# A transformer layer on one core: the queries of groups 2 to 6 in one two-level seven-product unit

## The chip, the core and the metric

The kernel runs on one core of a Trainium2 chip. The core has TensorE (PE in the profile; its weight loads are PEld), VectorE (DVE), ScalarE (ACT), GpSimd (POOL) and SyncE (SP), which issues nearly all DMAs here. The metric is device time in microseconds (us) of one execution; less is better.

## What is computed

One decoder layer on 1024 tokens of 512 features, all in fp32: attention with 32 query heads in 8 groups that share keys and values, rotary embedding, a causal softmax, an output projection, a layer norm; then a gated feed-forward part (1792 inner features) and a second layer norm.

```python
q = (x @ wq).reshape(B, T, H, HD).transpose(0, 2, 1, 3)      # T 1024, H 32, HD 128
k = (x @ wk).reshape(B, T, KV, HD).transpose(0, 2, 1, 3)     # KV 8
v = (x @ wv).reshape(B, T, KV, HD).transpose(0, 2, 1, 3)
q = q * cos + _rotate_half(q) * sin
k = k * cos + _rotate_half(k) * sin
scores = jnp.einsum('bhtd,bhsd->bhts', q, k) * (1.0 / np.sqrt(HD))
scores = jnp.where(mask, scores, -jnp.inf)                   # causal
att = jax.nn.softmax(scores, axis=-1)
out = jnp.einsum('bhts,bhsd->bhtd', att, v)
x = _layernorm(x + out.transpose(0, 2, 1, 3).reshape(B, T, H * HD) @ wo)
nx = x * rsqrt(mean(square(x)) + eps) * ln_w
x = _layernorm(x + (silu(nx @ gate_w.T) * (nx @ up_w.T)) @ down_w.T)
```

## The kernel before, in words

**Groups and tiles.** Attention runs group by group (`g`, 0 to 7). A group has four heads and 32 score steps: eight blocks of 128 tokens in the order `ORDER` = 7, 1, 5, 3, 4, 2, 6, 0 (the place in it is `p`), four steps of 32 tokens each (`b`). A step `t` holds 32 tokens of four heads on 128 partitions. `scores` (L590 to L618) multiplies the queries with the keys on PE into one of two PSUM pairs (`pair`, tag `ps_s`, 2 buffers); DVE adds the mask and takes the extreme (L590); ACT takes the exponential into a piece `p` of a pool of ten (L610), after which the pair is free; DVE inverts the sum (L614), ACT scales (L615), DVE transposes blocks of 32 by 32 into the buffer `xs` (L618, `turned` in the profile). After a tile's fourth step, `gather` issues 16 DMAs on SP (L668), which move that tile from `xs` to `ys` (`moved`). Tiles with even `p` use `xs` from its start, those with odd `p` its end. Then `Late` multiplies with the values (o), and for each pair of tiles `project_pair` multiplies with wo in a seven-product form (y), whose sums DVE adds into the result (L773).

**Filling.** All matmuls run in the order written (`keep_in_program_order`). Between two score steps, `run` places other work on PE by a planner's clock `now`, whose unit is a matmul of 512 columns: o and y of earlier tiles (`late`, available from a time `at` that counts the gather's issue and landing), and `early`, the projections of the next group, spread over all 32 steps. The other engines' order comes from a scheduler, unless an instruction is pinned.

**Projections.** `project_two` computes two heads of queries, or two groups' keys or values, for all 1024 tokens: x (features by tokens) is cut in two by features and by tokens, and so are the weights, and seven products of halves, each two matmuls of 512 columns, take the place of eight. Sums of the weights are made on POOL (`weigh`, L281 to L283), sums of x once at the start (s1 to s4). DVE adds the products from PSUM. A group's four query heads are two such steps, 28 matmuls of 512 columns. The rotary embedding follows as `chores` (`rotate_later`): two DVE steps with sin (L412), one with cos and a POOL sum (L417, L418); one chore is run at each score step. Queries lie in three rooms that turn (`held_q`), so that a group's second room can be filled while the first is read.

**The form at two levels in the FFN.** Gate and up projections already use, for units of four feature blocks, the seven-product form inside each of the seven products (`stages`, with `inner_sums` on DVE and `inner` on POOL): 49 matmuls of 256 columns, with copies of partial products from PSUM by ACT (L1440, L1441, L1445, L1448) and adds by DVE (L1458). Three products are interleaved.

**Loads.** `load(s)` brings the weights of step `s` two steps ahead into four buffers (`two_rows`), which the two halves of wo (`load_wo`) share; `weigh_wo` makes their sums on POOL (L315 to L318).

Of the kernel before, what the change touches and what calls it, by code (L numbers as in the profile page):

```python
# [28 lines left out]
F32 = mybir.dt.float32  # L29
BF16 = mybir.dt.bfloat16  # L30
AF = mybir.ActivationFunctionType
ALU = mybir.AluOpType
# [3 lines left out]
P = 128  # L36
# [4 lines left out]
KV = 8  # L41
HD = 128
REP = HEADS // KV
INNER = 1792
NT = T // P
NC = HID // P
NI = INNER // P
W = 512
Q = 32
B = P // Q  # L50
# [42 lines left out]
LEAST = 2  # L93


@with_exitstack
def kernel(
    ctx: ExitStack,
# [30 lines left out]

    cp = pool("cp", 10)  # L130

    ps_s = pool("ps_s", 2, space=PSUM)
    ps_m = pool("ps_m", 4, space=PSUM)

# [52 lines left out]
    with ExitStack() as att:  # L187
# [31 lines left out]
        held_q = qp.tile([P, 3, T // 2 // Q, REP, Q], F32, tag="q", name="queries")  # L219

        wvs, wks, wqs, wos, sums_of = {}, {}, {}, {}, {}
        of_kind = {"q": (wq, wqs), "k": (wk, wks), "v": (wv, wvs)}

        def load_weights(kind, which, parts=1):

            src, of = of_kind[kind]
            n = len(which)
            if kind == "k" and which == [1, 2]:

                t = held_q[:, 2].rearrange("p n h q -> p (n h q)")[:, :T]  # L230
            else:
                t = (rows if n == 1 else two_rows)(f"w{kind}{which[0]}")
            if kind == "k" and which == [KV - 1]:
                t = two_rows("wk_last")[:, :W]
            t = t.rearrange("p (c f) -> p c f", c=NC)
            size = n * HD // parts
            for k in range(parts):
                f0 = which[0] * HD + k * size
                nc.sync.dma_start(
                    t[:, :, k * size : (k + 1) * size],  # L240
                    src[:, f0 : f0 + size].rearrange("(c p) f -> p c f", p=P),
                )
                yield
            if kind == "k":


                with tc.issue_after(added.ins) if which == [1, 2] else ExitStack():
                    nc.gpsimd.tensor_scalar(t, t, -scale, 1.0, ALU.mult, ALU.mult)
            for k, w in enumerate(which):
                of[w] = t[:, :, k * HD : (k + 1) * HD]  # L250
# [18 lines left out]
        def weigh(s):  # L269


            if s >= len(steps):
                return
            kind, *which = steps[s]
            if len(which) < 2 or kind == "q" and which[0] // 2 in PLAIN:
                return
            a, b = (of_kind[kind][1][n] for n in which)
            b11, b21, b12, b22 = a[:, :2], a[:, 2:], b[:, :2], b[:, 2:]
            t = ap.tile([P, 2, NC // 2, HD], F32, tag="uq", name=f"uq{s}")
            u1, u2, u3 = t[:, 0], t[:, 1], b12  # L280
            nc.gpsimd.tensor_tensor(u1, b12, b11, ALU.subtract)  # L281
            nc.gpsimd.tensor_tensor(u2, b22, u1, ALU.subtract)
            nc.gpsimd.tensor_tensor(u3, b22, b12, ALU.subtract)  # L283
            sums_of[s] = b11, b21, b22, u1, u2, u3

        def difference(w):

# [176 lines left out]
        def project_two(s):  # L464


            b11, b21, b22, u1, u2, u3 = sums_of[s]
            u4 = b21
            kind, *which = steps[s]
            u = f"{kind}{which[0]}"  # L470
            v = ap.tile([P, W], F32, tag="v", bufs=1, name=f"sv{u}")

            def out(n, even):

                k = which[n]
                if kind == "q":
                    return queries(k // REP, even)[:, :, k % REP, :]
                if k not in (of := {"k": kTs, "v": vs}[kind]):
                    t = piece(f"{kind}{k}")
                    of[k] = t if kind == "k" else t.rearrange("p (j f) -> p j f", j=NT)  # L480
                t = of[k].rearrange("p (n q) -> p n q", q=P) if kind == "k" else of[k]
                return t[:, 1 - even :: 2, :]

            def done(n, even):

                if kind == "q":
                    rotate_later(out(n, even), even, f"{u}_{n}", even)
                elif kind == "k":
                    rotate_later(out(n, even), even, f"{u}_{n}", 2 * n)

            def put(dst, a, b):
                nc.vector.tensor_tensor(dst, alike(a, dst), b, ALU.add)

            ps = {}
            products = (
                (1, b11, a11), (2, b21, a12), (6, u2, s2), (5, u1, s1), (3, b22, s4),
                (7, u3, s3), (4, u4, a22),
            )
            for k, w, x in products:
                ps[k] = mbank(f"{u}_p{k}")  # L500
                if kind == "v":

                    for j in range(NT // 2):
                        for c in range(NC // 2):
                            matmul(
                                ps[k][:, j * P : (j + 1) * P],
                                lhsT=x[:, c, j * P : (j + 1) * P],
                                rhs=w[:, c],
                                start=c == 0,
                                stop=c == NC // 2 - 1,  # L510
                            )
                        if j == 1:
                            yield 1
                else:
                    for c in range(NC // 2):
                        matmul(
                            ps[k], lhsT=w[:, c], rhs=x[:, c], start=c == 0, stop=c == NC // 2 - 1
                        )
                        if c < NC // 2 - 1:
                            yield 1  # L520
                if k == 1:
                    nc.scalar.copy(v, ps[1])
                elif k == 2:
                    nc.gpsimd.tensor_tensor(u4, b21, u2, ALU.subtract)
                    put(c := out(0, 0), ps[2], alike(v, c))
                    done(0, 0)
                elif k == 6:
                    nc.vector.tensor_tensor(v, ps[6], v, ALU.add)
                elif k == 5:
                    put(c := out(1, 0), ps[5], alike(v, c))  # L530
                elif k == 3:
                    put(c := out(1, 0), ps[3], c)
                    done(1, 0)
                    if s:
                        weigh(s + 1)
                elif k == 7:
                    nc.vector.tensor_tensor(v, ps[7], v, ALU.add)
                    put(c := out(1, 1), ps[5], alike(v, c))
                    done(1, 1)
                else:  # L540
                    put(c := out(0, 1), ps[4], alike(v, c))
                    done(0, 1)
                    if s > 1:
                        load(s + 2)
                yield 1

        def projections(g):
# [6 lines left out]
                pieces += [(NC, project_keys(g, even)) for even in range(2)]  # L554
            for n in (2 * g, 2 * g + 1):
                s += 1
                if n in PLAIN:

                    which = (2, 0), (3, 0), (2, 1)
                    pieces += [(NC, project_queries(g, *which_of)) for which_of in which]  # L560
                else:
                    pieces.append((PAIR * 2, project_two(s)))
# [182 lines left out]
        def project_pair(g, k, oT):  # L745
# [13 lines left out]
            for n, (a, b) in enumerate(products):  # L759
                if n % 2 == 0:  # L760
                    y = mbank(f"y{g}_{k}_{n}").rearrange("p (n f) -> p n f", n=2)
                for h in range(2):
                    matmul(
                        y[:, n % 2, :],
                        lhsT=a[:, h * P : (h + 1) * P],
                        rhs=b[:, h, :],
                        start=h == 0,
                        stop=h == 1,
                    )
                if n % 2 or n == 6:  # L770
                    n0 = n - n % 2
# [10 lines left out]
        class Late:  # L782


            def __init__(self, g, i, y, at, unturned):
# [3 lines left out]
                else:  # L789
                    queue = max(at + TURNED, queue) + ISSUED  # L790
                    self.at = queue + LANDED
                self.g, self.weighed = g, False
                self.place = place(g, ORDER.index(i), i)
                self.left = self.units(g, i)
                self.work = self.pieces(g, i, y, unturned)
# [17 lines left out]
            def pieces(self, g, i, y, unturned):  # L813
# [41 lines left out]
                elif not first and keep:  # L855
                    held.append((PAIR, project_pair(g, k, both[g, k])))
                elif not first:
                    yield from project_pair(g, k, both[g, k])
                    if k == NT // 2 - 1 and g < KV - 2:
                        load_wo(g + 1)  # L860

# [75 lines left out]
        def run(g, until, early, pace, must=0, least=0, limit=None):  # L937
# [22 lines left out]
            while early.done < must:  # L960
                now += early.step()

        sums_of_x = [1, (s3, a11, a21), (s2, s1, a11)]
        for piece_of in (
            project_queries(0, 0, 0),
# [28 lines left out]
        for g in range(KV):  # L994
# [25 lines left out]
            for p, i in enumerate(ORDER):  # L1020
# [6 lines left out]
                    chores[0].append(lambda: nc.vector.tensor_tensor(s4, a12, s2, ALU.subtract))  # L1027
                if g == KV - 1 and p == 1:
                    load_wo(g)
                if g == 0 and 0 < p <= NT // 2:  # L1030
                    with tc.issue_after(cleared.ins):
                        if p == 2:
# [4 lines left out]
                for b in range(B):  # L1037
# [17 lines left out]
                    due += slot * weight[t]  # L1055
                    passed += weight[t]
                    done = p * B + b + 1
                    if g < KV - 2:
                        pace = early.total * min(1, passed / (slots - EARLIER))
                        must = early.total - MOST * max(0, slots - EARLIER - done)  # L1060
                        if g == 0:
# [688 lines left out]
```

## Time and profile before

| | |
|---|---|
| median of 2 runs | 1245.43 us (1245.15 to 1245.72) |
| the profiled execution | 1244.63 us, its span 1242.8 us |
| first scores of groups 1 to 7 | 161.8, 282.0, 403.2, 524.9, 646.1, 767.8, 872.5 us |
| PE busy | 1229.0 us, 99% of the span |
| DVE, ACT, POOL busy | 75%, 42%, 42% of the span |
| granted clock | 0.999 |

Rows of the profile name a line of the kernel, an engine, an operation and its tiles, written as out<-in; "x16" is the number of instructions. An fp32 matmul is two instructions. Line numbers in the groups are those of the kernel before; L137 is the helper through which every matmul goes, so PE's rows are told apart by their tiles: s scores, q_p, k_p and v_p projections, o, y, and in the FFN a, b, ab and c for the units. Matmuls are pipelined: the time of one row is longer than its share of a run of matmuls.

### The profile page before, as it was taken

What the parts mean: (1) busy time and instruction counts of PE and PEld (TensorE: products, weight loads), DVE (VectorE), ACT (ScalarE), POOL (GpSimd) and SP (SyncE); (2) the same over time, 40 slices, a digit from 0 to 9 for tenths busy, and PEclk for the clock granted to TensorE, in tenths of its full rate; (3) what the DMA queues carried; (4) which work ended last, traced back from release to release, by engine and by line L of the source; (5) the groups of instructions that cost most, each with busy time, mean ns of one, the idle gap of its engine ahead of it and who ended that gap; (6) DMA issues with size and microseconds to landing.
All of it is one profiled execution on the core that took longest, in us unless ns stands there. A gap on an engine that the chain in (4) does not pass through costs nothing. (4 is left out here: it accounts for less than half of the span.)

```text
span 1242.8 us, 14956 instructions
## 1 busy us (share of the span) xinstructions
PE 1229.0 (99%) x4336; PEld 770.6 (62%) x4336; DVE 935.2 (75%) x1891; ACT 524.9 (42%) x1075; POOL 516.7 (42%) x749
## 2 busy tenths in 40 slices
PE   9999999999999999999999999999999999999998
PEld 4645576566456755655567556554555758885887
DVE  5876787888788767878787678768766686889755
ACT  0443344444443444344444444544565137673000
POOL 5641334343424233424342424244240667779322
PEclk9999999999999999999999999999999999999999
DMA  8243325433543344434433433443453501140000
GB/s 279 53 117 77 82 63 147 104 83 78 136 106 88 81 130 96 99 80 118 102 94 80 124 92 90 99 126 95 113 117 91 135 18 52 51 136 18 17 18 35
DMA packets 84049, 115.58 MB, mean 93 GB/s; under 512 B 18304, under 2 KB 54912, under 8 KB 83968
## 3 DMA queue, kind: packets, MB, share of 16 engines
q1 hardware_dynamic: 82960, 112.66, 35.5%
q10 hardware_dynamic: 1008, 1.97, 0.4%
q8 instruction: 35, 0.57, 0.2%
q14 instruction: 46, 0.38, 0.1%
HBM read 37.23 MB, written 2.10 MB: 32 GB/s over the span
## 5 line engine op out<-in xcount | busy, mean ns | idle before, releaser
L610 ACT ACTIVATE p<-s,low 128x928 f32<-128x928 f32 (+31 forms) x256 | 179.2, 700 | 374.2 <-DVE low L590 361.9
L618 DVE STREAM_TRANSPOSE turned<-p 128x1024 f32<-128x1024 f32 (+7 forms) x244 | 187.3, 776 | 102.6 <-ACT p L615 68.3
L137 PE MATMUL o<-moved,v 128*128 128x512 f32 x550 | 254.6, 594 | 0.0
L615 ACT ACTIVATE p<-p,share 128x928 f32<-128x928 f32 (+31 forms) x256 | 188.0, 735 | 120.4 <-DVE share L614 120.3
L590 DVE CUSTOM_DVE_ANT_0 s<-s,mask 128x928 f32<-128x928 f32 (+31 forms) x256 | 179.1, 700 | 36.5 <-PE s L137 35.0
L137 PE MATMUL s<-k,queries 128*128 128x512 f32 (+15 forms) x576 | 204.0, 463 | 2.1 <-ACT p L610 2.1
L137 PEld LDWEIGHTS s<-k,queries 128*128 128x128 f32 x576 | 108.4, 190 | 110.5 <-issue 98.1
L137 PEld LDWEIGHTS o<-moved,v 128*128 128x128 f32 x550 | 102.4, 190 | 102.2 <-issue 95.3
L137 PE MATMUL q_p<-blocks,wq 128*128 128x512 f32 x260 | 124.5, 594 | 0.0
L605 POOL MEMSET p<- 128x96 f32 (+2 forms) x192 | 26.9, 151 | 230.4 <-DVE turned L618 209.6
L418 POOL TENSOR_TENSOR queries<-queries,q_b 128x512 f32<-128x512 f32 x52 | 71.5, 1375 | 116.6 <-DVE queries L417 107.7
L137 PE MATMUL y<-wo,oT 128*128 128x256 f32 x428 | 105.0, 382 | 0.7 <-ACT oT L848 0.7
L137 PEld LDWEIGHTS y<-wo,oT 128*128 128x128 f32 x428 | 79.4, 190 | 22.8 <-issue 7.9
L614 DVE RECIPROCAL share<-total 128x1 f32<-128x1 f32 x256 | 40.0, 156 | 61.1 <-ACT p L610 58.9
L412 DVE TENSOR_TENSOR q_b<-queries,sin 64x512 f32<-64x512 f32 x104 | 83.0, 798 | 3.1
L137 PEld LDWEIGHTS q_p<-blocks,wq 128*128 128x128 f32 x260 | 48.4, 190 | 45.9 <-issue 40.0
L137 PE MATMUL s<-kT,queries 128*128 128x512 f32 (+8 forms) x192 | 68.7, 466 | 1.8 <-ACT p L610 1.7
L773 DVE TENSOR_TENSOR sums<-y,sums 128x512 f32<-128x512 f32 x112 | 66.8, 605 | 3.1 <-PE y L137 2.0
L137 PEld LDWEIGHTS s<-kT,queries 128*128 128x128 f32 x192 | 35.7, 190 | 37.6 <-issue 29.2
L137 PE MATMUL y<-u,os 128*128 128x256 f32 x224 | 55.5, 384 | 0.8 <-POOL os L752 0.6
L137 PE MATMUL q_p<-blocks,uq 128*128 128x512 f32 x104 | 49.7, 592 | 0.0
L610 ACT ACTIVATION_READ_ACCUMULATOR p<-s,low 128x1 f32 x256 | 49.4, 193 | 0.0
(350 smaller groups left out, 1986.9 us busy)
## 6 DMA issues: line engine op xcount, KB each, us to landing
moved<-turned SPq DMA_DIRECT2D x112, 128.0 KB, 2.4
moved<-turned SPq DMA_DIRECT2D x128, 112.0 KB, 2.2
moved<-turned SPq DMA_DIRECT2D x112, 96.0 KB, 2.2
moved<-turned SPq DMA_DIRECT2D x112, 80.0 KB, 2.1
wo<-wo SPq DMA_DIRECT2D x16, 512.0 KB, 4.2
moved<-turned SPq DMA_DIRECT2D x128, 64.0 KB, 2.0
wq<-wq SPq DMA_DIRECT2D x14, 512.0 KB, 4.1
moved<-turned SPq DMA_DIRECT2D x128, 48.0 KB, 1.9
```

Source lines behind the costliest of these rows:

```text
L137: tc.keep_in_program_order(nc.tensor.matmul(*args, **kw))
L412: nc.vector.tensor_tensor(alike(b[0], dst)[to], dst[of], alike(sin[:, ts], dst)[of], ALU.mult)
L418: nc.gpsimd.tensor_tensor(dst, dst, alike(b[0], dst), ALU.add)
L590: extreme = nc.vector.tensor_tensor_reduce(out=s[:, :n], in0=s[:, :n], in1=mask[:, T - n :], scale=1.0, scalar=MASKED, op0=ALU.add, op1=AL ...
L605: cleared = nc.gpsimd.memset(p[:, n:full], 0.0)
L610: nc.scalar.activation(p[:, :n], s[:, :n], AF.Exp, bias=low, scale=-1.0, accum_out=total)
L614: nc.vector.reciprocal(share, total)
L615: last_of_all = nc.scalar.activation(p[:, :n], p[:, :n], AF.Copy, scale=share)
L618: nc.vector.transpose(x[:, :, :, b, :].rearrange("p b j q -> p j b q"), p[:, :full].rearrange("p (j b k) -> p j b k", b=B, k=Q),)
L773: pin(nc.vector.tensor_tensor(to, out, to, ALU.add))
```

## The change

Groups 2 to 6 (`UNITS`) no longer have `project_two` steps for their queries. In their place, after the 16th score step of the group before (`done == slots // 2`), `project_unit` computes all four heads in one run of 49 matmuls of 256 columns (seven products at two levels), with at most a few o steps between (`other`). The four inner sums that each of the seven operands of x needs are computed once, in group 0, on POOL (`keep_inner`, 28 sums of 256 columns) and written to DRAM (seven tiles of 128 by 1024). For each unit they are fetched again on SP (`fetch`): for the first three products into the first 3072 columns of `xs`, issued in program order after the 15th score step (`p == SETTLED`, `b == 2`); for products 7 and 5 into two pieces, issued at the unit's start; for products 3 and 4 again into `xs`, once products 1 and 2 have been read. The inner sums of the weights are made on POOL for every product (`inner_weights`, four sums of 128 columns; `weigh_unit`, three of 512). ACT copies partial products, DVE adds them into the queries; these are pinned to the program's order. The early work of the first half of such a group holds only the keys or values of the next, and has to be done by the 16th step; the second half has none. Weights for the next steps are loaded after the unit. The accumulation flags of value projections and of `project_pair` are set for the whole PSUM bank at its first product. `INNER` is renamed to `INTER`.

```diff
+UNITS = range(2, KV - 1)
+UNIT = 24.5
+SETTLED = 3
+INNER = (1, 2, 6, 7, 5, 3, 4)
...
+        def weigh_unit(g):
+            r1, r2 = (raw["q", REP * g + n] for n in (0, 2))
+            b11, b21, b12, b22 = r1[:, :2], r1[:, 2:], r2[:, :2], r2[:, 2:]
...
+            nc.gpsimd.tensor_tensor(u1, b12, b11, ALU.subtract)
+            nc.gpsimd.tensor_tensor(u2, b22, u1, ALU.subtract)
+            nc.gpsimd.tensor_tensor(u3, b22, b12, ALU.subtract)
...
@@ project_two, after its last product @@
                     if s > 1:
                         load(s + 2)
+                    if s % 3 == 1 and s // 3 + 1 in UNITS:
+                        weigh_unit(s // 3 + 1)
...
@@ projections @@
             for n in (2 * g, 2 * g + 1):
                 s += 1
+                if g in UNITS:
+                    continue
...
+        def keep_inner(k):
+            x, t = operand_of[k], piece(f"x{k}")
...
+            for to, a, b in ((k1, r12, r11), (k3, r22, r12), (k2, r22, k1), (k4, r21, k2)):
+                nc.gpsimd.tensor_tensor(to, a, b, ALU.subtract)
+            nc.sync.dma_start(inner_x[k], t)
...
+        def fetch(rooms, k):
+            nc.sync.dma_start(rooms[k], inner_x[k])
...
+        def stages(g, n, k, w, room, v):
...
+            mm(a[:, left], l11, r11, True)
+            mm(a[:, right], k3, x3)
+            yield
+            copy(v, a[:, right])
+            copy(a[:, right], a[:, left])
+            yield
...
+            mm(a[:, left], l12, r21)
+            mm(a[:, right], k2, x2)
+            copy(b[:, left], a[:, right])
+            yield
+            mm(a[:, right], k1, x1)
+            copy(b[:, right], a[:, right])
+            yield
+            mm(a[:, right], k4, r22)
+            mm(b[:, left], l22, x4)
...
+        def begin_unit(g, early):
+            if early:
+                rooms = (xs[:, n * T : (n + 1) * T] for n in range(3))
+                rooms_of[g] = dict(zip(INNER, rooms))
+                for k in INNER[:3]:
+                    fetch(rooms_of[g], k)
+                return
+            while current is not None:
+                chore()
+            weights_of[g] = [
+                inner_weights(g, k, ap.tile([P, W], F32, tag="rope_b", name=f"k{g}_{k}"))
+                for k in INNER[:2]
+            ]
...
+        def project_unit(g):
...
+            begin_unit(g, False)
...
+            for k in INNER[3:5]:
+                rooms[k] = piece(f"xk{g}_{k}")
+                fetch(rooms, k)
+            v = ap.tile([P, 3, W // 2], F32, tag="os", bufs=1, name=f"v{g}")
+            for n, k in enumerate(INNER):
+                begun.append(stages(g, n, k, weights[n], rooms[k], v[:, n % 3, :]))
+                for back in (0, 1, 0, 2, 1):
+                    if back <= n:
+                        next(begun[-1 - back])
+                    elif back == 2:
+                        other(1)
...
+                if n in (2, 3):
+                    k = INNER[n + 3]
+                    rooms[k] = rooms[INNER[n - 2]]
+                    fetch(rooms, k)
...
+            load(s + 3)
+            load(s + 4)
...
@@ the loop over a group's score steps @@
+                    if unit and p == SETTLED and b == 2:
+                        begin_unit(g + 1, True)
+                    if unit and done <= slots // 2:
+                        pace = early.total * min(1, done / (slots // 2 - EARLIER))
+                        must = early.total - MOST * max(0, slots // 2 - EARLIER - done)
+                        run(g, due, early, pace, must, LEAST)
+                        if done == slots // 2:
+                            due += UNIT
+                            project_unit(g + 1)
+                    elif g < KV - 2:
```

## The prediction

> **What bounds the kernel now.** I read the page's first part, then busy time by stretch for half groups, then the chain.
>
> ```profile
> PE 1229.0 (99%) x4336; PEld 770.6 (62%) x4336; DVE 935.2 (75%) x1891; ACT 524.9 (42%) x1075; POOL 516.7 (42%) x749
> ```
>
> ```profile
> core 0: us, PE busy (x) PEld busy (x) DVE busy (x) ACT busy (x) POOL busy (x), PEclk, DMA share, GB/s
> 403.20:465.00 61.80, 61.80 (x259) 39.78 (x259) 43.43 (x91) 28.12 (x55) 19.61 (x31) 1.00 0.43 107
> ...
> 465.00:524.90 59.90, 59.72 (x192) 34.90 (x191) 49.08 (x103) 25.69 (x54) 23.16 (x35) 1.00 0.39 93
> ```
>
> These are the first and second half of group 3 (four tiles each). TensorE has no gap: the kernel is as long as its matmuls. DVE is next, 49.08 of 59.90 us in the second half. So a matmul saved is time saved, if nothing makes TensorE wait; and a wait costs its full length, since there is no idle time that could take it up.
>
> **What is removed.** In the built order of the changed kernel, 140 query matmuls of 512 columns go (28 per group, five groups); 245 of 256 columns come (49 per unit), and 10 short ones with the mask. Their prices stand in the chain (start, length, what):
>
> ```profile
> 1001.95 1.72 PE pbu L137 x4
> 1003.66 1.72 PE pag L137 x4
> ...
> 1027.94 2.16 PE ab L137 x10
> ...
> 1037.01 2.16 PE ab L137 x10
> ```
>
> A 512-column fp32 matmul is two instructions; four take 1.72 us, so one matmul costs 0.86. The ab rows belong to units of the same form in the FFN: 9.07 us from one to the next, three products, 21 matmuls of 256 columns, 0.432 each. A unit is 49 x 0.432 = 21.2 us where 28 x 0.86 = 24.1 stood; two mask matmuls (bf16, each at most the 0.43 of a fp32 one) are taken at 0.3 together. Gain 24.1 - 21.2 - 0.3 = 2.6 per unit, **13 us** for five. The FFN units also show that TensorE, DVE and ACT can keep this pace: 104.00 of 104 us busy from 1021 to 1125.
>
> **What is added ahead of the unit: operands from DRAM.** The unit stands after the 16th of the group's 32 scores. Its first three products read their inner sums of x from the buffer `xs`, columns 0 to 3072: the room of the third tile (block 5) of the same group. They can only be fetched when that tile's 16 gather DMAs have read it, and SP issues everything in order. How long that takes is in the trace of before, group 3 (third tile's last score, its transpose, its gather, the fifth tile's first score):
>
> ```profile
> 447.88 1.45 PE L137 MATMUL s<-k,queries 128*128 128x512 f32 x4
> ...
> 452.82 0.98 DVE L618 STREAM_TRANSPOSE turned<-p 128x768 f32<-128x768 f32 x1 [0.38 <-ACT p L615]
> ...
> 453.86 10.40 SPq L668 DMA_DIRECT2D moved<-turned  x16
> ...
> 465.17 1.16 PE L137 MATMUL s<-k,queries 128*128 128x512 f32 x4
> ```
>
> ```profile
> moved<-turned SPq DMA_DIRECT2D x112, 96.0 KB, 2.2
> ...
> wo<-wo SPq DMA_DIRECT2D x16, 512.0 KB, 4.2
> ```
>
> Count from that score's start (447.88). The transpose ends at 5.9, the gather is issued from 6.0 to 16.4 (0.65 per DMA), its last DMA lands at 18.0 (2.2 after its issue). The first fetch can go at 16.8, when the 14th DMA has landed, and lands at **21.0** (4.2, as 512 KB of wo). The third goes at 18.0. Behind them in SP's order stands the fourth tile's gather, again 16 x 0.65 = 10.4, and only behind that the two fetches for products 7 and 5: issued at 28.9, landing at **33.1**.
>
> TensorE is earlier. From the same score to the unit it now has, in group 3 (s_t is the score of step t): s_23 1.28, y 1.71, v 1.95, and s_12 0.69, two o 1.71, s_13 0.75, s_14 0.80, s_15 0.85: 9.7 us. In before, 17.3 us lay between those scores, because query products filled them; those are what the unit takes away. It reaches the first fetched operand at 10.2 and waits to 21.0: 10.8 us. Up to product 7's operand the unit has 15 matmuls (6.4) and two masks (0.3), so without any wait it would be there at 16.4; the data is there at 33.1. **16.7 us** are lost by then, the first wait included. Group 1 has no y there (18.4 lost), groups 2 and 4 two key matmuls for v (16.9). Sum of five: 18.4 + 2 x 16.9 + 2 x 16.7 = **86 us**. Bounds: issues at 0.55, transfers at 3.7 (r from gate_t): 65; transposes ending at 7.4 (group 4), issues at 0.69, transfers at 5.4 (wd): 103. The refetches for products 3 and 4 follow at 29.8 and 35, land by 39.5, and are wanted from 39 and 42: covered.
>
> On POOL, the unit's weights take 28 sums of 128 columns (0.57 each in the FFN, L1244 to L1247: 0.46 to 0.70) and four of 512 (about 1.35), and the four sums of wo (1.27 each) stand amid them. The second query pair is loaded only after the last v or k product (issue near 5, landing 9 to 10). In groups 2 and 4 some 13 us of POOL work stand ahead of product 1's weights: about 22.5. That hides behind the same two fetches; if they came early, it would be the next wait.
>
> **What is added behind the unit: DVE.** From the end of product 5 to the end of the unit TensorE needs 5.1 us; in the built order DVE has 19 instructions between that point and the next score's minimum (7 adds from PSUM, 4 from SBUF, and of rotations 6 sin and 2 cos steps). By these rows of before, about 0.69 each:
>
> ```profile
> L412 DVE TENSOR_TENSOR q_b<-queries,sin 64x512 f32<-64x512 f32 x16 | 12.6, 786 | 0.5
> ...
> L417 DVE TENSOR_TENSOR queries<-queries,cos 128x512 f32<-128x512 f32 x9 | 6.5, 725 | 0.0
> L492 DVE TENSOR_TENSOR queries<-q_p,svq 128x512 f32<-128x512 f32 x8 | 5.4, 688 | 0.1
> ```
>
> That is 13.1 us, so the minimum of s_16 starts 8.0 after the unit's end and its exponential ends at 9.7 (0.85 + 0.75). TensorE has s_16, two o, s_17, two o: 5.4, and then needs that PSUM pair: **4.3 us**. Before the next minimum stand five more rotation steps (3.9): exponential at 14.5, TensorE ready at 12.5: 2.0 more. 6.3 per unit, **32 us**. Below: nothing, if rotations overlap better. Above: the rotations also wait for a buffer that POOL's add frees, and POOL stands behind the next k or v weights' DMA (4.2) and 5.7 us of its own sums: up to 14 per unit, 70. In the second half as a whole TensorE has 40 us of work and DVE, counted by the same rows, about as much, so DVE cannot catch up quickly.
>
> **Clock.** The longest idle of TensorE in mid-run is 1.1 us, with no slower matmul after it; but the first ones after launch were slow, 561 ns for 379:
>
> ```profile
> L137 PE MATMUL idle<-turned 128*128 128x256 f32 x10 | 3.9, 561 | 1.2 <-DVE turned L366 1.2
> ```
>
> 10 x 0.18 = 1.8 us for a cold start. Waits of 5 to 10 us may bring that back: 0 to 3 times per unit; I take once, **9 us**, ends 0 and 27.
> [...]
>
> **Elsewhere.** Group 0 gets 28 sums of 256 columns on POOL (0.72 each, L752: 20 us) and seven writes; its scores start 5.0 us or more after the exponential that frees their pair, and blocks of 5.8 stand ahead of a memset: 0 to 8, taken as 0. ACT has four copies of 256 columns per product (0.36 to 0.39), 1.5 in 3.0 us, as in the FFN. The changed start flags add no instruction.
>
> **Sum**, against the profiled execution (1244.6 us, span 1242.8; the median of the runs is 1245.43, 0.8 above): 1244.6 - 13 + 86 + 32 + 9 = **1359 us**, 9% slower.
>
> **Rivals.** *The unit runs as in the FFN*, its operands there in time: 1244.6 - 13 = 1232, 1% faster, within what a measurement can tell (2%). For it: the FFN's gapless units, and 35 fetches of 512 KB against a DMA share of 0.43. Against: it needs the third tile's gather landed 11 us earlier; every group of before shows it 17.6 to 19.1 us after the score. It decides if TensorE comes to the unit later than about 21 us (33 for product 7). Chance 0.06. *Only the first wait is paid* (10.8 or 12.5 us; products 7 and 5 in time, DVE caught up): 1232 + 56 = 1288. It would need SP to issue those fetches ahead of the fourth gather; the built order says otherwise. 0.14. *DVE and POOL bind behind the unit*, 14 us each: 1359 + 38 = 1397; DVE's share of the second half speaks for it. 0.14. The forecast: 0.66.
>
> **Numbers.** Range 1285 to 1405: from the second rival to the third with part of the slower bounds. Over 2% faster 0.01, within 2% 0.06, slower 0.93.
>
> **What would show it.** Right: in groups 1 to 5 TensorE idle before a_ and a_7 matmuls, released by a DMA of inner_x, some 10 and 5 us long; SP's fetches issued right after a gather's last landing; score matmuls after the unit waiting for ACT's p, and behind it DVE; a half group of about 100 us with the unit. Wrong: o matmuls idle instead, or PE still at 99%. What would make the sum wrong most easily is the transpose of the third tile ending earlier, or gathers issued faster than 0.55 us each.

## The result and the profile after

The changed kernel takes **1430.62 us** (median of 2 runs, 1427.69 to 1433.55) where the kernel before took 1245.43: the ratio is **1.1487**, 95% interval 1.1385 to 1.1589. The profiled execution took 1433.55 us, its span is 1431.5, 188.7 us longer than the span before. The direction was forecast; the size was not: 1359 was predicted, and 1405 was the upper end of the range.

The first part of the page of the kernel after, and from its second part PE's busy tenths and the clock granted to it:

```profile
PE 1272.0 (89%) x4556; PEld 829.6 (58%) x4556; DVE 974.6 (68%) x1926; ACT 568.2 (40%) x1210; POOL 603.9 (42%) x897
...
PE   9999995799778986799579977898999999999998
...
PEclk9999997899899998999899989999999999999999
```

PE was at 99% and is at 89%. The loss lies in slices 7 to 28 (215 to 1002 us), the five groups that hold a unit and the one behind them; there the granted clock falls too. PE is busy for 43 us more although it has less to do: a matmul at a lower clock counts as busy for longer (behind a wait 0.43 us per instruction of 256 columns for 0.216). Busy time by stretch shows this for the two halves of group 3 (the same stretches as in the prediction; the unit is in the first):

```profile
core 0: us, PE busy (x) PEld busy (x) DVE busy (x) ACT busy (x) POOL busy (x), PEclk, DMA share, GB/s
472.90:577.50 104.60, 85.26 (x359) 60.24 (x358) 49.31 (x102) 39.41 (x86) 30.53 (x60) 0.93 0.47 125
577.50:630.10 52.60, 42.61 (x137) 25.34 (x136) 48.76 (x95) 22.78 (x48) 24.43 (x29) 0.94 0.21 53
```

Before, PE had no gap in 61.8 and 0.2 us of gaps in 59.9 us. Now it stands still for 19 of 104.6 and 10 of 52.6 us. In the second half DVE is busy for 48.76 of 52.60 us, so it has hardly any room there.

**Where the 188.7 us went.** I split the length of every half group in three: idle time of PE (gaps over 0.05 us), the time its matmuls would take at full rate (0.216 us per instruction of 256 columns, in proportion for other widths; the rate can be read in a fence below), and the rest, which is what the matmuls took longer than that. Groups 1 to 6, after minus before:

| term | predicted | measured |
|---|---|---|
| matmul work at full rate | -13 | -13.1 |
| idle, first halves of groups 1 to 5 (ahead of and in the unit) | +86 | +90.3 |
| idle, second halves of groups 1 to 5 (behind the unit) | +32 | +47.2 |
| idle in group 6 | none | +8.5 |
| matmuls below full rate | +9 | +55.8 |
| sum | +114 | +188.7 |

Three terms hold the miss: the slow matmuls (47 us), the waits of the second halves (15) and group 6 (8.5). The 47.2 us of the second halves are of two kinds: 35.7 stand right behind the unit, before the third and fourth score steps of the half (s_18 and s_19), where the prediction had its 32; 11.5 stand near the end, a wait of 2.30 us in each group that it did not have.

**Ahead of the unit**, group 3 again, from the timeline of the kernel after (start, length, engine, line, what; in brackets the idle time before it and what ended it):

```profile
520.51 1.45 PE L144 MATMUL s<-k,queries 128*128 128x512 f32 x4
...
525.31 0.98 DVE L647 STREAM_TRANSPOSE turned<-p 128x768 f32<-128x768 f32 x1 [1.00 <-ACT p L644]
...
526.31 10.12 SPq L697 DMA_DIRECT2D moved<-turned  x16
...
536.75 1.61 SPq L1016 DMA_DIRECT2D turned<-inner_x  x3
...
538.42 13.34 SPq L697 DMA_DIRECT2D moved<-turned  x16
...
540.23 1.19 PE L144 MATMUL a<-turned,k 128*128 128x256 f32 x2 [8.44 <-DMA turned<-inner_x]
...
541.43 1.06 PE L144 MATMUL ab<-blocks,wq 128*128 128x256 f32 x2
542.30 1.19 PE L144 MATMUL ab<-turned,k 128*128 128x256 f32 x2
...
546.62 0.59 PE L144 MATMUL ab<-blocks,wq 128*128 128x256 f32 x2
547.06 0.59 PE L144 MATMUL ab<-turned,k 128*128 128x256 f32 x2
...
551.87 1.01 SPq L1016 DMA_DIRECT2D xk<-inner_x  x2
```

This is the predicted chain: third tile's transpose, sixteen gather DMAs, three fetches right behind, the fourth tile's sixteen DMAs, the fetches for products 7 and 5. From the start of s_23 (520.51) the first fetch is issued at 16.2 and landed at 19.6 (predicted 16.8 and 21.0), product 7's at 31.4 and 35.4 (predicted 28.9 and 33.1). The "ab" rows with `wq` give the rate, from one start to the next: two instructions take 0.87 us right behind the wait (541.43 to 542.30) and 0.44 six us after it (546.62 to 547.06).

**Behind the unit**, DVE and PE at the start of the second half (timeline; s_16 starts at 577.48):

```profile
581.72 1.13 DVE L436 TENSOR_TENSOR q_b<-queries,sin 64x512 f32<-64x512 f32 x1
582.88 1.10 DVE L1078 TENSOR_TENSOR queries<-queries,v 128x512 f32<-128x512 f32 x1
584.01 2.23 DVE L436 TENSOR_TENSOR q_b<-queries,sin 64x512 f32<-64x512 f32 x2
586.27 1.10 DVE L441 TENSOR_TENSOR queries<-queries,cos 128x512 f32<-128x512 f32 x1
587.41 1.10 DVE L436 TENSOR_TENSOR q_b<-queries,sin 64x512 f32<-64x512 f32 x1
588.43 0.71 DVE L619 CUSTOM_DVE_ANT_0 s<-s,mask 128x544 f32<-128x544 f32 x1
...
590.19 2.07 PE L144 MATMUL s<-k,queries 128*128 128x512 f32 x2 [6.95 <-ACT p L639]
```

The minimum of s_16 starts 10.9 us after s_16 on PE (predicted: 8.0), and s_18 waits 6.95 us for its PSUM pair (predicted: 4.3). Its first two instructions then take 2.07 us, where two of that width take 1.02 at full rate. The rotation steps shown cost 1.10 to 1.13 us each, not 0.69.

**Near the end of the second half**, PE again in group 3:

```profile
622.46 1.81 PE L144 MATMUL s<-k,queries 128*128 128x512 f32 x6
626.57 0.73 PE L144 MATMUL s<-k,queries 128*128 128x64 f32 x4 [2.30 <-ACT p L639]
```

The second score step of the last tile waits for the exponential of the score two before it. In the kernel before, 12 instructions of y and 6 of o (5.2 us) are placed between these same scores; in the changed order none are, because the second half has no projection work left. That the wait comes with the unit is shown by the last run below, where group 5 has no unit and no idle time; that this order is the reason is read from the rows, and no run changes it.

**In group 6** (timeline: PE, then SP), a wait that the prediction doesn't have:

```profile
994.94 1.88 PE L144 MATMUL q_p<-blocks,uq 128*128 128x512 f32 x4
1004.67 2.04 PE L144 MATMUL y<-wo,oT 128*128 128x256 f32 x4 [7.85 <-DMA wo<-wo]
...
1000.40 1.07 SPq L326 DMA_DIRECT2D wo<-wo  x2
```

In the kernel before, 22.3 us of other matmuls lay between the last y of group 5 and the first of group 6 (798.4 to 820.7), and wo for group 6 was loaded and summed in them. Now 3.4 us lie there (993.3 to 996.7).

### The profile page after: what moved, and what is told of

Its sections match the earlier page's. It is cut to its first block, busy times and chain, and to the rows that moved or that the text cites. A ratio compares the mean times of both kernels' runs of the same rounds, so it can differ in the third digit from the quotient of the medians.

```text
span 1431.5 us, 15861 instructions
## 1 busy us (share of the span) xinstructions
PE 1272.0 (89%) x4556; PEld 829.6 (58%) x4556; DVE 974.6 (68%) x1926; ACT 568.2 (40%) x1210; POOL 603.9 (42%) x897
## 5 line engine op out<-in xcount | busy, mean ns | idle before, releaser
L144 PE MATMUL o<-moved,v 128*128 128x512 f32 x550 | 267.2, 621 | 1.9 <-DMA moved<-turned 1.1
L144 PE MATMUL s<-k,queries 128*128 128x512 f32 (+15 forms) x576 | 211.8, 484 | 53.9 <-ACT p L639 53.8
L647 DVE STREAM_TRANSPOSE turned<-p 128x1024 f32<-128x1024 f32 (+7 forms) x244 | 183.2, 769 | 48.1 <-ACT p L644 38.9
L144 PEld LDWEIGHTS o<-moved,v 128*128 128x128 f32 x550 | 105.7, 199 | 104.8 <-issue 96.6
L436 DVE TENSOR_TENSOR q_b<-queries,sin 64x512 f32<-64x512 f32 x104 | 86.8, 835 | 4.9 <-POOL queries L442 1.8
L878 ACT COPY oT<-o 128x512 f32<-128x512 f32 x58 | 33.7, 581 | 117.5 <-PE o L144 117.0
L1078 DVE TENSOR_TENSOR queries<-ab,queries 128x512 f32<-128x512 f32 x40 | 25.7, 685 | 63.9 <-PE ab L144 63.9
L144 PE MATMUL a<-turned,k 128*128 128x256 f32 x60 | 23.4, 478 | 48.0 <-POOL k L1029 28.3
L1043 ACT COPY ab<-ab 128x256 f32<-128x256 f32 x60 | 21.6, 360 | 75.7 <-PE ab L144 75.0
```

What stands on the lines that cost most here:

```text
L144: tc.keep_in_program_order(nc.tensor.matmul(*args, **kw))
L436: nc.vector.tensor_tensor(alike(b[0], dst)[to], dst[of], alike(sin[:, ts], dst)[of], ALU.mult)
L647: nc.vector.transpose(x[:, :, :, b, :].rearrange("p b j q -> p j b q"), p[:, :full].rearrange("p (j b k) -> p j b k", b=B, k=Q),)
L878: nc.scalar.copy(oT, o)
L1078: ordered(nc.vector.tensor_tensor(to, x, y, ALU.add))
```

## The experiments

Each time is that of one execution unless an interval is given; the kernel before took 1245.1 to 1245.7 us beside them (medians). The two executions of the kernel after lie 5.9 us apart, so differences of a few us are read from the stretches of the profiled executions and not from the total. "Idle" and "below full rate" are the terms of the table above, for groups 1 to 5; the kernel after has 90.3 and 30.6 us in the first halves, 48.0 and 28.4 in the second.

### Which of the two makes product 1 late: the fetch or POOL's sums

Three kernels take away the fetches, the weight sums, and both.

```diff
 e1: nothing is fetched, rooms are quarters of resident operands
-            nc.sync.dma_start(rooms[k], inner_x[k])
+            rooms[k] = blocks[:, INNER.index(k)].rearrange("p c f -> p (c f)")
 e2: raw slices of the weights in place of their sums
-                ordered(nc.gpsimd.tensor_tensor(to, a, b, op))
+            k1, k2, k3, k4 = l21, l11, l12, l22
 e3: both
```

> The unit reads quarters of resident tiles of x in place of the fetched inner sums, and nothing is fetched (the queries are then not the reference's). In the changed kernel (1431 us in its profile) TensorE waits at product 1 about 9 us and at product 7 about 5 us per unit, each followed by some 5 us at half clock. Theory, the fetches behind SP's gathers set both waits: the wait at product 7 goes (5.0 + 2.4 us of slow clock, five units: 37 us); at product 1 POOL's weights are the next limit: in groups 2 and 4 they are ready at 19 to 20 us after s_23, as late as the fetch, so the wait stays there, and in groups 1, 3 and 5 it shrinks to 1 to 3 us (some 20 us in all). About 1375 us. Rival, POOL's weights alone set the first wait, as the releasers in the waits name them: only the second wait goes, 1394 us, and product 1 starts at 20 us in every group. Rival, the transfers slow other DMAs down or contend: more than 60 us are gained.

> The fetches stay; POOL makes no sums of query weights for the unit (raw quarters are used, so the queries are not the reference's). Theory, the fetch lands at 20 us after s_23 whatever POOL does: product 1 waits until then in every group and product 7 until about 34; nothing gained in the first half but waits of 0.5 to 1 us inside the unit, and a few us behind it, where POOL's adds of the rotations come earlier: 1415 to 1430 us. Rival, POOL sets the first wait: product 1 starts at about 11 us after s_23 and the first wait of 9 us goes; the second then grows by as much, and the time stays near 1425, but the wait has moved from product 1 to product 7.

> Neither fetches nor sums of query weights on POOL (queries not the reference's): the unit finds its operands. Theory: no wait of more than 2.5 us at its start (ACT's chain of the last scores, about 2), none at product 7; 85 of the 90 us of idle TensorE in the first halves of groups 1 to 5 go, less 10 that the start costs, and two cold starts per unit (2.7 us each, 27 us): 1431 - 75 - 27 = about 1330 us. The waits for scores behind the unit (48 us in all, and their cold start) stay. Rival, TensorE cannot run the unit beside attention (ACT's and DVE's queues): waits of 5 us or more remain inside the unit, 1370 us or more.

Measured: **1386.3**, **1430.6** and **1363.5 us**. Without sums nothing is gained: the fetches alone make the unit wait (idle in first halves 91.2). Without fetches the second wait is gone in every group and the first shrinks to 3 to 6 us in groups 1, 3 and 5, but not in groups 2 and 4. PE's costliest rows for product operands in a stretch of group 2, first of the kernel without fetches, then of the one without sums (count, busy us and mean ns, idle before and what ended it):

```profile
L144 PE MATMUL a<-blocks,k 128*128 128x256 f32 x24 | 8.0, 415 | 9.2 <-POOL k L1030 8.7 <-ACT b L1044 0.4
```

```profile
L144 PE MATMUL a<-turned,wq 128*128 128x256 f32 x12 | 4.7, 484 | 9.5 <-DMA turned<-inner_x 9.0 <-ACT b L1038 0.4
L144 PE MATMUL a<-xk,wq 128*128 128x256 f32 x6 | 2.4, 491 | 5.8 <-DMA xk<-inner_x 5.8
```

In groups 2 and 4 both come at the same time (in the kernel after, the first sum of product 1 is ready 19.9 and 20.2 us after s_23, the fetch has landed at 19.8 and 19.9), so taking away either leaves the other. The prediction had POOL at 22.5 there, hidden behind the fetch as "the next wait": that it is. With both gone the kernel is still 33 us above what I had put: 34.4 us of idle stay in the first halves, and nothing of either sort touches the second halves (51.4 idle).

### The wait behind the unit: the flush of the rotations

The code has a cause for it that I had not used. At the fifth tile all rotations queued for the second room are run at once (`4: (1,)` in the loop over `chores`). In a group with a unit, its own twelve steps for that room are in the queue by then. This kernel empties the queue before the unit instead; its output is the same.

```diff
-                for n in {0: (0,) if g % 2 else (0, 2), 4: (1,)}.get(p, ()):
+                for n in {0: (0,) if g % 2 else (0, 2), 4: () if g + 1 in UNITS else (1,)}.get(p, ()):
 ...
+                            while chores[1]:
+                                current = current or chores[1]
+                                chore()
                             project_unit(g + 1)
```

> The only edit: the rotations still queued for the second room of queries are run before the unit, and no more at the fifth tile, where in the changed kernel the unit's own 12 rotation steps are all run ahead of the first score (the output is the reference's). Theory, those steps on DVE make the waits for scores behind the unit (9 to 10 us per unit, and 2.8 us of slow clock after): they fall to 1 to 3 us; 5 x (7 + 2.8) = 49 us less, about 1382 us. Rival, DVE is short of time in the whole second half (its busy time is 48 of 53 us there), so the waits only move to later scores: less than 20 us gained, over 1410 us.

Measured: **1385.4 us**, 45 less. Busy time by stretch for the two halves of group 3 in this kernel (columns as above):

```profile
451.80:554.50 102.70, 85.13 (x356) 60.37 (x357) 54.94 (x112) 39.71 (x87) 35.95 (x63) 0.93 0.47 125
554.50:598.70 44.20, 41.35 (x138) 25.48 (x136) 40.06 (x86) 22.71 (x48) 17.73 (x26) 0.96 0.27 68
```

The second half falls from 52.6 to 44.2 us; over five groups idle falls from 48.0 to 11.9 and the time below full rate from 28.4 to 17.0. The waits before s_18 and s_19 (35.7 us) are gone: they were the flush. What stays are the waits of 2.3 to 2.7 us before the second score step of the last tile, one in each group.

### The clock: keeping PE busy while it waits

If a wait costs a slow stretch behind it, then repeating a matmul during the wait should shorten the kernel, though nothing arrives earlier.

```diff
             mm(a[:, left], l11, r11, True)
+            for _ in range({1: 36, 7: 20}.get(k, 0)):     # second run: {1: 18, 7: 10}
+                mm(a[:, left], l11, r11, True)
             mm(a[:, right], k3, x3)
```

> The changed kernel with PE kept busy where it waited inside the unit: the first matmul of product 1 is issued 36 more times into the same place before the one that needs the first fetch, and that of product 7 20 more times (280 matmuls more, 216 ns each at full rate; the output stays the same). The theory is that a wait of some 5 us or more is paid twice: for itself and for a stretch of about 5 us at half rate behind it, 2.9 us lost behind the first and 2.4 us behind the second wait of group 2. The fetches land when they did, so the waits end when they did; only the slow stretches behind them should go: 5 units by 5.3 us, 1430 to about 1404, although PE does 60 us more work; clock lost in the first halves of groups 1 to 5 from 39 us to under 10 us. Rival, that the lower clock comes of something else than the waiting (how much PE does altogether, or the small matmuls): 1430 or, with the added work in the way, above.

Measured: **1459.7 us**, 29 more, because I had counted 216 ns for a matmul that is two instructions of 216: the filling ran 15.5 and 8.6 us, far past the ends of the waits. It still answers the question. Busy time by stretch for the first half of group 3, with 36 and 20 and then with 18 and 10 repeats:

```profile
478.80:586.80 108.00, 104.54 (x471) 79.05 (x470) 48.42 (x101) 39.49 (x86) 30.72 (x60) 1.00 0.45 119
```

```profile
466.30:568.70 102.40, 94.65 (x415) 69.33 (x414) 48.34 (x101) 39.43 (x86) 30.67 (x60) 0.98 0.47 125
```

The clock is 1.00, and the time below full rate in the first halves falls from 30.6 to 6.1 us. Where all operands are there (behind the too long filling of group 2) the unit takes 6.3 us from product 2 to product 7 and 18.7 from product 5 to s_16; in the kernel after it takes 8.1 and 20.5.

> The first filling run again with the fill sized right: that run showed that one of the filling matmuls issues as two of 216 ns, so 36 and 20 of them ran 16 and 9 us, past the ends of the waits. Now 18 before product 1's fetched operand (7.8 us for a wait of 8.8 in group 2) and 10 before product 7's (4.3 us for a wait of 5.0); the output stays the same. From the fill's end to the end of the unit that run was faster than the changed kernel by 2.4 us behind the first wait and 2.3 behind the second (group 2). If the slow stretch is what a wait costs beside itself, 5 units by 4.7 us go: 1430.6 to about 1407, with idle time in the first halves of groups 1 to 5 down by some 60 us, though nothing is waited for a moment less. Rival: what is gained behind the waits is lost again to the scores, which DVE paces: 1425 to 1430.

Measured: **1424.3 us**, 6 less (9 less than the profiled execution of the kernel after); the first halves together shrink from 510.0 to 499.2 us, not by the 23.5 expected, and the rival (1425 to 1430) is nearer. The slow time did go, from 30.6 to 14.5. But idle time and filling together take 95.5 us where 90.3 were idle, and further on the unit waits again: from product 2 to product 7 group 2 takes 8.4 us, no less than the 8.1 of the kernel after, because the third fetch lands only at 25.1. **A slow stretch ahead of a fixed arrival cost nothing here; it only filled part of the next wait.** So the 30.6 us of the first halves are slow time that is there, but about 11 of it are what a cure of the clock alone gives back.

### The order on SP: fetches on another queue

> The changed kernel with the fetches for products 7 and 5 issued from ACT's queue instead of SP's, where they stood behind the sixteen DMAs of the fourth tile's gather. If it is the queue that makes product 7 late, the wait before it (5 us in each of groups 1 to 5) and the slow stretch behind it (2.4 us) go: 5 by 7.4 us, 1430 to about 1394. Rivals: POOL's weights for product 7 end only just before the fetch, and then at most half of it goes (about 1410); or the transfer itself, beside the gather's, is what is late, and nothing goes (1430).

```diff
-                fetch(rooms, k)
+                (nc.scalar).dma_start(rooms[k], inner_x[k])     # products 7 and 5
```

Measured: **1421.6 us**, 9 less where 37 were expected. The wait before product 7 is gone, but the one before product 1 has grown from between 8.4 and 10.8 us to between 12.5 and 15.3. Idle time in the first halves is hardly changed (88.5 us for 90.3): the one wait is as long as the two were. What is gained is the slow stretch behind the second (19.0 us below full rate for 30.6). The first fetch is issued on SP 21.3 us after s_23 in group 2 instead of 16.5, though nothing was put ahead of it on SP. The second run under "All three cures together" shows why.

### What the unit costs without its operands and without the flush

> Neither fetches nor weight sums in the unit (operands from a resident tile, slices of the weights as they lie: the seven-product form's inner sums on both sides are left out), and the second room's rotations run before the unit instead of behind it. What is left of the change is the unit's order of matmuls, copies and additions. If the two cures add (77 us below 1430.6 together from the earlier pair of runs, and 45 us from the flush alone): 1363.5 - 45 = about 1318. If the form itself were as good as its count of matmuls says, with nothing to wait for, it would come to about 1245 - 13 = 1232 and the idle time that the third run still had at the unit's start (6 to 8 us in each group) would have to go with the flush.

The edits of the third and fourth kernel together. Measured: **1310.6 us**, somewhat better than the sum of the parts. It is still 65 us above the kernel before: some 48 us of idle (7.4 per first half, 2.4 per second half), 9 in group 6, 23 below full rate, less 13 of work saved. PE's waits in group 2 of this kernel (us in total, times, longest):

```profile
PE a L144 <- ACT a L1039: 4.4, 1, 4.4
PE s L144 <- ACT p L633: 3.5, 3, 2.3
PE ab L144 <- DVE queries L1074: 2.2, 2, 1.1
```

ACT's copies between the products, the scores' exponentials and DVE's additions are waited for. The form as built, amid another group, doesn't run gapless as the FFN's units do.

### All three cures together

> The changed kernel with three edits at once, output the same: rotations ahead of the unit (45 us less by the run that had it alone), the fetches for products 7 and 5 on ACT's queue (37 us less if that theory holds), and the filling matmuls before product 1's fetched operand only (2.9 us in each of five units, 14). Sum: 1430.6 - 45 - 37 - 14 = about 1335. It would still be slower than before, by the first wait (9 us in each unit), group 6's wait for wo (8 us) and what the unit's start costs beside.

Measured: **1368.7 us**, ratio 1.0988 (1.0953 to 1.1023). Idle falls to 23.1 us in the first halves and 4.8 are below full rate, but the time stands in the filling (36 repeats, 15.5 us per unit), and the wait is as long as that: with both fetches on ACT's queue the first fetch on SP lands at 25.2 us after s_23 in group 2, not at 19.8. The term of 37 us had failed in the run with that edit alone, where it gave 9; those 28 us are most of the miss.

> The changed kernel with three edits, output the same: rotations ahead of the unit (45 us less by the run that had it alone); only product 7's fetch on ACT's queue (the run with product 5's there too had ACT stand before it until its room came free, ahead of the copies that product 1 needs); 18 filling matmuls before product 1's fetched operand. Sum: 1430.6 - 45 - 5 times 2.4 behind the first wait - 5 times 5.0 to 7.4 for the second: 1337 to 1349. If ACT's queue is held up by product 7's room as well, the second term turns to nothing or below: 1370 and more. Either way slower than before, as long as the first wait stands.

Measured: **1367.9 us**, ratio 1.0984 (1.0962 to 1.1005), the rival's side. Its timeline and waits (SP's queue) for group 3, s_23 at 490.7, where the kernel after had its s_23 at 520.5:

```profile
496.48 13.04 SPq L697 DMA_DIRECT2D moved<-turned  x16
509.85 1.58 SPq L1016 DMA_DIRECT2D turned<-inner_x  x3
...
503.50 0.33 ACTq L1016 DMA_DIRECT2D xk<-inner_x  x1
```

```profile
SPq L697 <- DMA xk<-inner_x: 2.9, 1, 2.9
```

The third tile's gather took 10.12 us to issue and takes 13.04. It waits on SP for the landing of the fetch on ACT, which it has nothing to do with. The semaphores in the built order and in the trace have the reason: DMAs of both queues use eight of them in turn, and each DMA waits until the one that used its semaphore before has landed. In the trace of the kernel after, a load of wq goes out on SP at 5.62, when a load of x that ACT had issued with the same semaphore has landed at 5.60; and in group 3 the gather's DMA at 544.90, when the third fetch, eight DMAs before it, has landed at 544.88. Here the fetch on ACT lands at 507.73, 4.2 us after its issue; the gather's DMA that has the same semaphore is issued at 507.75. The gather's issues stand still from 13.6 to 17.1 us after s_23, and the first fetch on SP goes 3 us later. What the second wait gives, the first takes. The kernel after pays the same in its own order: there the waits of SP's queue have 2.1 us in group 3 for the gather behind the three fetches, which makes product 7's fetch 2.5 us later than I had it.

### One part alone, and one unit less

```diff
-UNITS = range(2, KV - 1)
+UNITS = ()                      # second run: range(2, KV - 2)
```

> No group is given the unit: what is left of the change is the part of group 0 that forms x's inner sums on POOL and writes them to DRAM (28 subtractions, 7 writes of 512 KB, never read back), and the start flags. The prediction put it at nothing, with 8 us as its upper bound. By that 1245 to 1246; by the bound 1253.

Measured: **1246.24 us** against 1245.5, ratio 1.0006 (0.9996 to 1.0016): group 0's sums, their seven writes and the start flags cost nothing that can be measured.

> The unit for groups 2 to 5 only, so group 5 runs as before. If each unit pays its own waits and nothing else, group 5 falls from 155.7 to about 121.8 us: 1430.6 - 34 = 1397, with group 6's wait for wo (7.9 us) where it was. If that wait is there because the unit in group 5 changes which work is left over for group 6, it goes too with its slow stretch: about 1386.

Measured: **1385.0 us**, 45.6 less. Busy time by stretch for groups 5 and 6 of this kernel, then of the kernel after:

```profile
781.70:902.40 120.70, 120.70 (x451) 74.78 (x450) 84.76 (x181) 53.59 (x107) 36.19 (x62) 1.00 0.40 98
902.40:1012.40 110.00, 107.94 (x321) 59.11 (x320) 83.02 (x183) 53.71 (x109) 41.49 (x65) 1.00 0.44 107
```

```profile
784.60:940.30 155.70, 128.67 (x494) 85.90 (x494) 95.28 (x196) 62.26 (x134) 53.79 (x89) 0.92 0.38 101
940.30:1061.00 120.70, 110.15 (x323) 59.89 (x323) 78.94 (x175) 54.27 (x109) 37.87 (x66) 0.97 0.41 99
```

Group 5 falls by 35 us and group 6 by 10.7, its wait for wo included. So that wait belongs to the unit in group 5: with it the planner leaves other work over for group 6, and the two projections that need different wo come to stand 3.4 us apart, where this kernel has 20.6 us of other matmuls between them (935.6 to 956.1). A unit costs about 35 us where it stands, and the last one 11 more behind it.

No version beat the kernel before. Even with free operands and the flush moved, the form is at 1310.6, so a better order of the fetches alone would not do.

## Why the prediction was wrong

**What held.** *The work*: 13 us, to 0.1 (the two mask matmuls of a unit, taken at 0.3 us together, take 0.21 and 0.11 in group 3, from their start to the next row's). *The waits ahead of the unit*: 86 predicted, 90.3 measured, and the chain is the one it named. That the sums agree so well is in part luck. The waits before products 1 and 7 are 72 of the 90.3; the other 18 us are short waits of up to 1.2 us, 10 us of it for DVE's additions inside the unit, and the prediction had none of these because it took the FFN's gapless units as proof that the engines keep pace. Two errors of a few us lie in the chain itself: the gathers go a little faster than 0.65 per DMA, and the fourth one is held up by the semaphores of the fetches (2.1 us in group 3). *POOL as the next wait*: shown by the kernel without fetches. *Group 0 at nothing*: shown by the part alone.

**"10 x 0.18 = 1.8 us for a cold start", "I take once, 9 us"** is the term that failed most: 56 us. Both of its factors were wrong. There are three waits long enough in each unit (before products 1 and 7 and behind the unit), and each brought the slow rate back; I had taken one. And the price was from the wrong row: the first matmuls after launch took 561 for 379 ns, but the rows after a wait show half rate, 0.43 for 0.216 us per instruction, for 4.9 to 5.9 us in group 2 (3.5 at the least, in group 5), 2.3 to 2.9 us lost each time. That is some 8 us per unit, 40 in five. Of the rest, about 8 us stand behind the waits of 2.30 us at the ends of the second halves (0.4 and 0.5 lost in groups 2 and 3, but 1.9 to 3.6 in groups 1, 4 and 5) and 2 behind the wait in group 6. My upper bound of 27 was three restarts of 1.8, so the range could not hold it. What the slow stretches are worth is less than their sum: about 11 of the first halves' 30.6 us came back when only the clock was mended.

**"That is 13.1 us, so the minimum of s_16 starts 8.0 after the unit's end"** belongs to the second: 32 predicted, 47 measured. The waits that this step speaks of came to 35.7, but by two errors that nearly cancel. The 19 instructions were counted rightly; their price was not, and the minimum starts 10.9 us after the unit's end in group 3. So s_18 waits 5.3 to 7.0 us, not 4.3; the next wait, taken at 2.0, is 0.5 to 1.8. The price of 0.69 is what a rotation step takes when POOL does nothing. In the kernel after, sin and cos steps take 0.69 alone; those with POOL sums beside them all the time take about 1.10 in most cases, and behind the unit POOL's sums of weights and of `os` run all the time. The mean of 786 ns in the row that I quoted already held this. And I took the rotations' place in DVE's order as given, where one line of the code puts them there; moving it took away these waits, three quarters of all idle time in the second halves, so they were a cost of the change that could be avoided. The other 11.5 us, near the end of the second halves, had no term at all: the prediction went no further than the first waits behind the unit.

**"Elsewhere"** had no term for what the planner does with the work behind a unit. The wait for wo in group 6, 8.5 us and about 2 of slow matmuls, was in the built order of PE, where two projections with different wo stand 3.4 us apart. The prediction went through the order around the unit alone.

## What to carry to other kernels

A kernel with PE at 99% has no room for waits. Here each new wait of 4.4 to 10.8 us cost its own length and 1.7 to 3.2 us of slow matmuls behind it, except where another wait followed that the slow stretch only ate into: price new waits so. Price DVE's work by rows from a place where POOL is as busy as it will be (a rotation step took 0.69 us alone and about 1.10 beside POOL's sums). And when a block of work is moved to another place in a hand-written order, look for what is flushed, loaded or left over at fixed points behind it, one whole group further on.

## What was not expected of the hardware

- In the kernel after, PE's rate was halved behind waits of 4.4 to 10.8 us, for some 3.5 to 6 us (1.7 to 3.2 us lost). Single waits of 1.1 us or less left no such stretch; those of 2.30 us left one in groups 1, 4 and 5 (1.9 to 3.6 us lost) and hardly any in groups 2 and 3 (0.4 and 0.5). With matmuls repeated during the wait it did not come: the granted clock was then 1.00 in the first half of group 3, where it was 0.93.
- DVE's steps with two operands in SBUF took 0.68 to 0.69 us alone (at 574.40 and 575.85 in group 3, with POOL idle) and mostly about 1.10 with POOL sums beside them all the time; next to longer sums single steps took up to 1.7. Behind the unit in group 3 it was about 1.14 from one step to the next over five steps in a row, beside sums of 1.05 to 1.17.
- An issue on one queue waited for a DMA of another: 2.9 us on SP for a fetch that ACT had issued, by the eight semaphores that the DMAs of both queues use in turn.
